# Reworking the head of a two-block kernel: angles, small softmax passes, weight sums and loads

## The chip, the core and the metric

The kernel runs on one core of one Trainium2 chip. The metric is the device time of one execution in microseconds, the median of the runs. Engines are named as in the profile: PE (matmul; PEld is its weight load), DVE (VectorE), ACT (ScalarE), POOL (GpSimd) and SP (SyncE, which issues all DMA). Everything is float32.

## What is computed

Input: 32 sequences of 64 tokens with 512 features, positions, and one condition vector of 512 per sequence. Two blocks follow one another:

```python
# block 0
h = rms_norm(x) * (ln1_w * (1 + cond @ ln1_tw.T))      # per sequence
q, k, v = h @ Wq.T, h @ Wk.T, h @ Wv.T                 # 8 heads of 64, one key/value head
q, k = rope(q, pos), rope(k, pos)                      # angles = pos * 1/10000**(i/32)
x = x + softmax(q k.T / 8) v @ Wo.T
h = rms_norm(x) * (ln2_w * (1 + cond @ ln2_tw.T))
x = x + (silu(h @ Wg.T) * (h @ Wu.T)) @ Wd.T           # 512 -> 2048 -> 512
# block 1
scale, shift = split(cond @ W_ada.T + b_ada)
h = layer_norm(x) * (1 + scale) + shift
q = h @ Wq1.T                                          # 16 heads of 32
c = h @ Wkd.T                                          # latent of 128
k, v = c @ Wku.T, c @ Wvu.T                            # 4 key/value heads
x = x + softmax(rope(q) rope(k).T / sqrt(32)) v @ Wo1.T
```

Attention stays within a sequence of 64 tokens in both blocks. The rope of block 0 takes its positions from the input; that of block 1 uses constant tables.

## The kernel before

Tokens are cut into eight units of 256 (four sequences). A unit lies in SBUF as 128 partitions by 4 feature chunks by 256 tokens. Each unit goes through `attention0` (block 0's attention, and at its end the normed input of the MLP), `mlp`, and `attention1` (block 1).

**MLP.** The three weight matrices (gate, up, down) are cut into eight groups each; every unit goes through these 24 groups in turn. A group is multiplied as a 2 by 2 block product with seven products instead of eight (`SEVEN`). That takes four sums of weight quarters per group. In unit 0, `combine` makes them (lines 211 to 213 on DVE, 214 on POOL; the tile is called `set`, the fourth quarter `a`), and `done_with` stores them (line 219) in a DRAM tile `kept`, called `sums` in the profile. Units 1 to 7 load them from there (line 204). Sets lie in a ring of `MW` = 4 buffers, `a` in a ring of two. `first_products` and `last_products` are gate and up (`gu`, line 723); lines 737, 739, 742 and 749 add the products into `u`, `w` and `c` on DVE, lines 760 to 764 multiply the two, and `down` is line 782.

**Activations.** The seven-product scheme needs sums of the input too: `h` and `hc`, lines 570 to 573, at the end of `attention0`, behind h times the inverse root `r_b` (line 565; 374 is the root on ACT, 375 the reciprocal on DVE).

**Angles.** `angles(u0)` makes sine and cosine of two units' positions, 128 columns at a time: it splits the angle in two parts by the factor 4097, multiplies each by pieces of 1/(2 pi) (line 305), and takes the fraction after each product by adding and subtracting a large constant (`ROUND`, line 300; 301 subtracts, 311 adds up), so that Sin (lines 317, 318) gets a small argument. Line 319 puts the sign on. All but the two Sin runs on DVE. `tables` spreads the result by matmul (`tab`, line 327) and scales it by the inverse root `r_a` to `cs` (lines 333, 334). `angles(0)` runs in the head, `angles(2)` at the end of unit 1's attention0, `angles(4)` and `angles(6)` in the attention0 of units 3 and 5. Note that unit 1's attention0 runs partly in the head too.

**Softmax.** `softmax` works on 128 rows by 8 groups of 64 keys: maximum (line 426), subtract (428), Exp (429), sum (431) and reciprocal (432), then p times sm on POOL (433). `turned` transposes p on PE (`pp`, line 439), ACT copies it (`pT`, 440), `cx` is p times v (549, 692), copied as `cT` (558, 701), and `output` projects it (`po`, line 402 of `project`) and adds x on DVE (452).

**Order.** Jobs are generators that yield planned costs; `Order.run` interleaves them. The head (attention0 of units 0 and 1, with the condition's projections between) and the tail (attention1 of units 6 and 7) are "lean": there one works with more buffers and shares work out, since no MLP runs beside it. In between, `mlp(u)` runs together with attention0 of unit u+1 and with attention1 of earlier units. A scheduler then fixes each engine's instruction order. DMA is all issued by SP in order. The weights of block 1 and x of units 2 to 4 are asked for when the head has been built:

```python
    for w, key in ((wq1, "wq1"), (wkd, "wkd"), (wkv1, "wkv1"), (wo1, "wo1")):
        nc.sync.dma_start(w, a[key])
    for u in range(2, XB):
        load_x(u)
    combine(0)
    combine(1)
```

In `attention1`, line 598 multiplies h by the scale on POOL, 602 multiplies by the inverse root `r_c` on DVE and 603 adds the shift on POOL. The last weight group of the down product and both tail jobs close the kernel; the last `output` stores two halves of unit 7.

Of the kernel before, what the change touches and what calls it, by code (L numbers as in the profile page):

```python
# [17 lines left out]
P = 128  # L18
# [27 lines left out]
ROUND = 12582912.0  # L46
TWO_PI = float(np.nextafter(np.float32(2 * np.pi), np.float32(0)))
# [44 lines left out]
def two_blocks(ctx: ExitStack, tc: tile.TileContext, a: dict, out: bass.AP):  # L92
# [31 lines left out]

    spread = fixed("spread", [P, US, P])
# [11 lines left out]
    nc.gpsimd.memset(eps1, EPS1)  # L137

# [68 lines left out]
    def combine(n):  # L207

        if n < len(sequence) and sequence[n][1] < NP:
            t, a21 = sets[n], odd[n]  # L210
            nc.vector.tensor_tensor(t[:, 0], a21, t[:, 6], ALU.add)
            nc.vector.tensor_tensor(t[:, 1], t[:, 0], t[:, 4], ALU.subtract)  # L212
            nc.vector.tensor_tensor(t[:, 2], t[:, 4], a21, ALU.subtract)
            nc.gpsimd.tensor_tensor(t[:, 3], t[:, 5], t[:, 1], ALU.subtract)

    def done_with(m, q):
        n = place[m, q]
        if q < NP:
            nc.sync.dma_start(kept[3 * (q % NP) + m], sets[n][:, 0:4])
        load_sets(n + 1 + MW)  # L220
# [58 lines left out]
    def angles(u0):  # L279

        cols = slice(u0 * S, (u0 + 2) * S)

        def some(tag, name, cols=512, bufs=2):
            return work(tag, [P, cols], f"{name}_{u0}", bufs)[:, : 2 * S]

        posi = positions.pop()
        posf, sign = some("u", "posf"), some("v", "sign")
        ang, lo, hi, prod = some("p0", "ang"), some("p0", "lo"), some("pT0", "hi", 512, 1), some("r0", "prod", UT, 1)
        acc, rnd = angle[:, 0, cols], angle[:, 1, cols]
        nc.vector.tensor_copy(posf, posi)  # L290
        nc.vector.tensor_scalar(sign, posf, 0.0, None, ALU.is_ge)
        nc.vector.tensor_scalar(sign, sign, 2.0, -1.0, ALU.mult, ALU.add)
        nc.vector.tensor_tensor(posf, posf, sign, ALU.mult)
        nc.vector.tensor_scalar(ang, posf, freq, None, ALU.mult)
# [4 lines left out]
        def fraction(dst, src):  # L299
            nc.vector.tensor_scalar(rnd, src, ROUND, ROUND, ALU.add, ALU.subtract)  # L300
            nc.vector.tensor_tensor(dst, src, rnd, ALU.subtract)

        first = True
        for piece, turn in ((hi, 0), (hi, 1), (lo, 0), (hi, 2), (lo, 1)):
            nc.vector.tensor_scalar(prod, piece, TURN[turn], None, ALU.mult)
            if first:
                fraction(acc, prod)
                first = False
            else:
                fraction(prod, prod)  # L310
                nc.vector.tensor_tensor(acc, acc, prod, ALU.add)
        nc.vector.scalar_tensor_tensor(acc, lo, TURN[2], acc, ALU.mult, ALU.add)
        nc.vector.scalar_tensor_tensor(acc, ang, TURN[3], acc, ALU.mult, ALU.add)
        fraction(prod, acc)
        nc.vector.tensor_scalar(lo, prod, 0.25, None, ALU.add)
        fraction(hi, lo)
        nc.scalar.activation(acc, hi, AF.Sin, scale=TWO_PI)
        nc.scalar.activation(rnd, prod, AF.Sin, scale=TWO_PI)
        nc.vector.tensor_tensor(rnd, rnd, sign, ALU.mult)
# [79 lines left out]

    def project(ps, w, cols, h):  # L400
        for k in range(KC):
            nc.tensor.matmul(ps, w[:, k, cols], h[:, k, :], start=(k == 0), stop=(k == KC - 1))  # L402
# [18 lines left out]
    def softmax(sc, scale, name, p):  # L421
# [6 lines left out]
        nc.vector.tensor_tensor(p3, s3, mx.unsqueeze(2).to_broadcast(heads), ALU.subtract)  # L428
        nc.scalar.activation(p, p, AF.Exp, scale=scale)
        sm = work("sm", [P, 8], f"sm_{name}", 2)  # L430
        nc.vector.tensor_reduce(sm, p3, AX.X, ALU.add)  # L431
# [11 lines left out]
    def output(u, cT, w, name, last=False):  # L443

        x = x_units[u]
        for h in range(2):
            po = abank(f"po_{name}_{h}").rearrange("p (c t) -> p c t", c=2)
            for c in range(2):
                o = 2 * h + c
                project(po[:, c], w, slice(o * P, (o + 1) * P), cT)  # L450
            part = slice(2 * h, 2 * h + 2)
            nc.vector.tensor_tensor(x[:, part], x[:, part], po, ALU.add)  # L452
            yield 3.4, 2.0 * h
# [5 lines left out]
    def attention0(u, room, early=None, late=None):  # L459
# [48 lines left out]
        for i, part in enumerate((a_, b_)):  # L508
            for hh in range(2):
                to = slice((2 * i + hh) * HALF0, (2 * i + hh + 1) * HALF0)  # L510
                ins = [t[part].rearrange("p (b s) -> p b s", s=S) for t in (ku, kw)]
                nc.vector.tensor_tensor(kb[to, :, hh, :], *ins, ALU.add)
# [14 lines left out]
        for t in range(2):  # L527
# [12 lines left out]
            ps.append(softmax(sc, HD0**-0.5, f"0_{u}_{t}", space(room, "p", 512, f"p0_{u}_{t}")))  # L540
# [24 lines left out]
        nc.vector.tensor_tensor(h, h, all_chunks(r), ALU.mult)  # L565
# [14 lines left out]
    def attention1(u, room):  # L580
# [13 lines left out]
        nc.vector.tensor_tensor(h, x, all_chunks(mean), ALU.subtract)  # L594
        sq = tile4(room, "h", f"sq1_{u}") if lean else work("sq", [P, KC, UT], f"sq1_{u}", 1)
        nc.scalar.activation(sq, h, AF.Square)
# [5 lines left out]
        nc.vector.tensor_tensor(h, h, all_chunks(r), ALU.mult)  # L602
        nc.gpsimd.tensor_tensor(by_seq(h), by_seq(h), per_seq(t1, u), ALU.add)
# [62 lines left out]
        def scores(t, h_):  # L666
# [12 lines left out]
            return softmax(sc, HD1**-0.5, name, space(room, "p", 512, f"p{name}"))  # L679
# [128 lines left out]

    def mlp(u):
        for q in range(u * NP, (u + 1) * NP):  # L810
            gate = first_products(0, q)
# [26 lines left out]
    def early():  # L838
        angles(0)
        for z in (kblk0[0], vblk0[0], kblk0[1], vblk0[1], *vblk1):  # L840
            nc.gpsimd.memset(z, 0.0)
# [25 lines left out]
    for w, key in ((wq1, "wq1"), (wkd, "wkd"), (wkv1, "wkv1"), (wo1, "wo1")):  # L867
        nc.sync.dma_start(w, a[key])
    for u in range(2, XB):
        load_x(u)  # L870
# [137 lines left out]
```

## Time and profile before

| what | value |
|---|---|
| median of three runs | 1091.65 us (1091.65 to 1093.0) |
| profiled execution | 1091.63 us, its span 1089.9 us, mean granted PE clock 0.989 |
| busy: PE, PE loads | 1033.7 us (95%), 951.4 us (87%) |
| busy: DVE, POOL, ACT | 586.3 us (54%), 432.5 us (40%), 317.6 us (29%) |
| DMA | 198.45 MB, mean 182 GB/s |
| head, 0 to 78 us | PE busy 60.2 us |
| tail, 1048 to 1090 us | PE busy 34.4 us |

Span is the time between the first and the last instruction of the profiled execution. A line of the timeline gives start, length, engine, source line, operation, out<-in with sizes, and in brackets the idle time before it with the instruction that ended it. "x8" says that eight instructions were drawn together.

### The profile page before, as it was taken

The page shows a single profiled execution, that of the slowest core. Times are in us where ns is not written, and L with a number is a line of the kernel's source. Part 1 is how long each engine was busy: PE and PEld are TensorE (multiplying, and loading weights), DVE is VectorE, ACT ScalarE, POOL GpSimd, SP SyncE. Part 2 cuts the span into 40 slices and gives each one's busy share as a digit, 9 for nine tenths or more (in the row PEclk, how much of TensorE's full clock was granted, in tenths as well). Part 3 has the DMA queues.
Part 4 walks back from the last instruction along what each step waited for, and adds up shares of the span by engine and source line. Part 5 has one row for each costly group of instructions (what it writes and reads, how often), then busy time and mean ns, then how long its engine had stood idle before and what let it go on. Part 6 is the DMA issues. An engine that isn't in the chain of part 4 may idle for free.

```text
span 1089.9 us, 20180 instructions
## 1 busy us (share of the span) xinstructions
PE 1033.7 (95%) x7940; PEld 951.4 (87%) x7940; DVE 586.3 (54%) x1362; ACT 317.6 (29%) x648; POOL 432.5 (40%) x509
## 2 busy tenths in 40 slices
PE   6799899999999999999999998999999999999898
PEld 4679899989999988998988997998999989998776
DVE  5977566554455468333675249443465354235553
ACT  2231022244314234223333222144314242122422
POOL 2334444444245345225434235434335334245531
PEclk9899999999999999999999999999999999999999
DMA  9426786525666264555555374445655266762001
GB/s 332 190 84 205 261 280 221 203 103 204 214 217 218 105 227 180 186 188 203 181 195 186 132 271 162 137 169 203 220 205 204 102 228 217 281 232 79 1 20 39
DMA packets 68109, 198.45 MB, mean 182 GB/s; under 512 B 7216, under 2 KB 15152, under 8 KB 67504
## 3 DMA queue, kind: packets, MB, share of 16 engines
q1 hardware_dynamic: 68016, 197.17, 51.4%
q8 instruction: 63, 1.03, 0.4%
q14 instruction: 30, 0.25, 0.1%
HBM read 180.37 MB, written 16.78 MB: 181 GB/s over the span
## 4 chain that ended last, share of the span: by engine, by line
PE 74%; DVE 9%; DMA 8%; POOL 2%; ACT 2%; issue 2%; SPq 0%; ACTq 0%; DVEq 0%; POOLq 0%
PE gu L723 29%; PE down L782 15%; PE po L402 9%; PE q L402 9%; DMA set<-sums 5%; DMA set<-in_wmlp 3%; PE sc L671 2%; PE pp L439 2%; PE lat L402 1%; PE sc L533 1%; PE cx L549 1%; PE cx L692 1%; PE kv L402 1%; DVE sm L431 1%; PE tab L327 1%
## 5 line engine op out<-in xcount | busy, mean ns | idle before, releaser
L723 PE MATMUL gu<-h,set 128*128 128x128 f32 x2048 | 290.7, 277 | 16.1 <-DVE c L742 6.3
L723 PEld LDWEIGHTS gu<-h,set 128*128 128x128 f32 x2048 | 260.2, 192 | 26.6 <-issue 12.8
L723 PE MATMUL gu<-hc,set 128*128 128x128 f32 x1536 | 215.4, 276 | 2.7 <-DVE set L212 1.9
L723 PEld LDWEIGHTS gu<-hc,set 128*128 128x128 f32 x1536 | 193.2, 193 | 5.2 <-DVE set L212 2.8
L761 POOL TENSOR_TENSOR act<-c,c 128x384 f32<-128x384 f32 x64 | 63.8, 997 | 232.6 <-DVE c L749 152.6
L782 PE MATMUL down<-td,set 128*128 128x128 f32 x1024 | 138.4, 278 | 3.2 <-DMA set<-sums 2.6
L782 PEld LDWEIGHTS down<-td,set 128*128 128x128 f32 x1024 | 126.5, 194 | 5.4 <-issue 3.0
L782 PE MATMUL down<-act,set 128*128 128x128 f32 x768 | 109.8, 278 | 1.8 <-DMA set<-in_wmlp 1.7
L735 ACT COPY e<-gu 128x128 f32<-128x128 f32 x128 | 33.8, 265 | 266.7 <-PE gu L723 266.6
L402 PE MATMUL po<-cT,wo 128*128 128x256 f32 x480 | 109.8, 381 | 1.4 <-ACT cT L558 1.4
L749 DVE TENSOR_TENSOR c<-gu,u 128x256 f32<-128x256 f32 x128 | 53.7, 422 | 104.9 <-PE gu L723 104.0
L782 PEld LDWEIGHTS down<-act,set 128*128 128x128 f32 x768 | 98.2, 192 | 8.2 <-issue 3.5
L737 DVE TENSOR_TENSOR u<-e,gu 128x128 f32<-128x128 f32 x128 | 35.7, 280 | 126.0 <-ACT e L735 125.6
L402 PEld LDWEIGHTS po<-cT,wo 128*128 128x128 f32 x480 | 89.3, 191 | 13.9 <-ACT cT L558 2.1
L419 POOL TENSOR_TENSOR qT<-u_q,v_q 128x512 f32<-128x512 f32 x30 | 38.1, 1269 | 113.1 <-DVE v_q L418 108.3
L433 POOL TENSOR_TENSOR p<-p,sm 128x512 f32<-128x512 f32 x40 | 42.0, 1059 | 98.5 <-DVE sm L432 79.8
L818 ACT ACT_TABLE_LOAD x33 | 42.3, 1283 | 68.4 <-DVE c L749 68.1
L402 PE MATMUL q<-h,wqkv 128*128 128x256 f32 x256 | 60.2, 387 | 0.2 <-ACT r_a L374 0.2
L452 DVE TENSOR_TENSOR x<-x,po 128x512 f32<-128x512 f32 x32 | 22.0, 687 | 71.0 <-PE po L402 71.0
L402 PEld LDWEIGHTS q<-h,wqkv 128*128 128x128 f32 x256 | 48.2, 194 | 7.1 <-issue 0.6
L402 PE MATMUL q<-h,wq 128*128 128x256 f32 x224 | 50.7, 379 | 0.1
L763 POOL TENSOR_TENSOR td<-act 128x256 f32<-128x256 f32 x64 | 47.5, 742 | 4.8
(226 smaller groups left out, 1443.8 us busy)
## 6 DMA issues: line engine op xcount, KB each, us to landing
set<-sums SPq DMA_DIRECT2D x168, 512.0 KB, 5.5
set<-in_wmlp SPq DMA_DIRECT2D x192, 384.0 KB, 4.6
sums<-set SPq DMA_DIRECT2D x24, 512.0 KB, 3.0
mod<-in_mod SPq DMA_DIRECT2D x8, 512.0 KB, 10.0
x<-in_x SPq DMA_DIRECT2D x8, 512.0 KB, 9.2
out_x<-x SPq DMA_DIRECT2D x16, 256.0 KB, 2.0
a<-in_wmlp SPq DMA_DIRECT2D x24, 128.0 KB, 2.5
wo<-in_wo SPq DMA_DIRECT2D x2, 1024.0 KB, 11.0
```

Of the source, the lines that this page charges most:

```text
L402: nc.tensor.matmul(ps, w[:, k, cols], h[:, k, :], start=(k == 0), stop=(k == KC - 1))
L419: nc.gpsimd.tensor_tensor(dst, cut(u, every), cut(v, every), ALU.add)
L433: nc.gpsimd.tensor_tensor(p3, p3, sm.unsqueeze(2).to_broadcast(heads), ALU.mult)
L452: nc.vector.tensor_tensor(x[:, part], x[:, part], po, ALU.add)
L723: nc.tensor.matmul(ps, w[:, slot, k * P : (k + 1) * P], b[of][:, k], start=start and k == 0, stop=k == 1, skip_group_check=True)
L735: nc.scalar.copy(e, ps[:, 0])
L737: nc.vector.tensor_tensor(u2, e, ps[:, 1], ALU.add)
L749: nc.vector.tensor_tensor(c.rearrange("p (a b) t -> p a b t", b=2)[:, :, 1], ps[:, 2:4], u2.unsqueeze(1).to_broadcast([P, 2, HT]), ALU.add,)
L761: nc.gpsimd.tensor_tensor(act[:, 1:4], gate[:, 1:4], c[:, 1:4], ALU.mult)
L763: nc.gpsimd.tensor_tensor(td[:, 0:2], act[:, 1:3], act[:, 0:2], ALU.subtract)
L782: nc.tensor.matmul(sums_of[u][p][:, c], w[:, slot, c * P : (c + 1) * P], b[of], start=q % NP == 0 and i % 2 == 0 and c == 0, stop=q % NP = ...
L818: nc.scalar.activation(gate[2][:, 0], gate[0][:, 0], AF.Silu)
```

## The change

- Eleven matmuls of 128x128 on the constant `ones` stand first on PE (`WARM`).
- `combine` of the first two sets runs on POOL; each `combine` issues the store of its sums itself.
- `angles` has 12 DVE operations and ten on ACT; products, rounding and summation run over five pieces at once; the cosine comes from Sin with a bias of pi/2, the sign from ACT.
- `by_row` shares h times r between DVE and POOL in lean units; the mean's subtraction and the shift of `attention1` are cut in halves there, and half of `kblk` goes to POOL.
- `softmax` of the second tile of lean units: the maximum, times minus the scale, is the bias of eight Exp of 128x64, which also sum up.
- The last output goes in four parts instead of two.
- Weights of block 1 and x of units 3 and 4 are asked for within the list of the MLP's products.

```diff
+WARM = 11
...
+    idle = bank("at", "idle")
+    for _ in range(WARM):
+        nc.tensor.matmul(idle[:, :P], ones, ones, start=True, stop=True)
...
             t, a21 = sets[n], odd[n]
-            nc.vector.tensor_tensor(t[:, 0], a21, t[:, 6], ALU.add)
-            nc.vector.tensor_tensor(t[:, 1], t[:, 0], t[:, 4], ALU.subtract)
-            nc.vector.tensor_tensor(t[:, 2], t[:, 4], a21, ALU.subtract)
+            e = nc.gpsimd if n < 2 else nc.vector
+            e.tensor_tensor(t[:, 0], a21, t[:, 6], ALU.add)
+            e.tensor_tensor(t[:, 1], t[:, 0], t[:, 4], ALU.subtract)
+            e.tensor_tensor(t[:, 2], t[:, 4], a21, ALU.subtract)
             nc.gpsimd.tensor_tensor(t[:, 3], t[:, 5], t[:, 1], ALU.subtract)
+            m, q = sequence[n]
+            nc.sync.dma_start(kept[3 * q + m], t[:, 0:4])
 
     def done_with(m, q):
-        n = place[m, q]
-        if q < NP:
-            nc.sync.dma_start(kept[3 * (q % NP) + m], sets[n][:, 0:4])
-        load_sets(n + 1 + MW)
+        load_sets(place[m, q] + 1 + MW)
...
         nc.vector.tensor_copy(posf, posi)
-        nc.vector.tensor_scalar(sign, posf, 0.0, None, ALU.is_ge)
-        nc.vector.tensor_scalar(sign, sign, 2.0, -1.0, ALU.mult, ALU.add)
-        nc.vector.tensor_tensor(posf, posf, sign, ALU.mult)
-        nc.vector.tensor_scalar(ang, posf, freq, None, ALU.mult)
+        nc.scalar.activation(ang, posf, AF.Abs, scale=freq)
         nc.vector.scalar_tensor_tensor(lo, ang, 4097.0, ang, ALU.mult, ALU.subtract)
         nc.vector.scalar_tensor_tensor(hi, ang, 4097.0, lo, ALU.mult, ALU.subtract)
         nc.vector.tensor_tensor(lo, ang, hi, ALU.subtract)
 
-        def fraction(dst, src):
-            nc.vector.tensor_scalar(rnd, src, ROUND, ROUND, ALU.add, ALU.subtract)
-            nc.vector.tensor_tensor(dst, src, rnd, ALU.subtract)
...
-        for piece, turn in ((hi, 0), (hi, 1), (lo, 0), (hi, 2), (lo, 1)):
-            nc.vector.tensor_scalar(prod, piece, TURN[turn], None, ALU.mult)
...
-                fraction(prod, prod)
-                nc.vector.tensor_tensor(acc, acc, prod, ALU.add)
+        for k, (piece, turn) in enumerate(((hi, 0), (hi, 1), (hi, 2), (lo, 0), (lo, 1))):
+            nc.scalar.mul(prods[:, k], piece, TURN[turn])
+        nc.vector.tensor_scalar(rnds, prods, ROUND, ROUND, ALU.add, ALU.subtract)
+        nc.vector.tensor_tensor(prods, prods, rnds, ALU.subtract)
+        nc.vector.tensor_reduce(acc, prods.rearrange("p k c -> p c k"), AX.X, ALU.add)
         nc.vector.scalar_tensor_tensor(acc, lo, TURN[2], acc, ALU.mult, ALU.add)
         nc.vector.scalar_tensor_tensor(acc, ang, TURN[3], acc, ALU.mult, ALU.add)
-        fraction(prod, acc)
-        nc.vector.tensor_scalar(lo, prod, 0.25, None, ALU.add)
-        fraction(hi, lo)
-        nc.scalar.activation(acc, hi, AF.Sin, scale=TWO_PI)
-        nc.scalar.activation(rnd, prod, AF.Sin, scale=TWO_PI)
-        nc.vector.tensor_tensor(rnd, rnd, sign, ALU.mult)
+        nc.vector.tensor_scalar(rnds[:, 0], acc, ROUND, ROUND, ALU.add, ALU.subtract)
+        nc.vector.tensor_tensor(f, acc, rnds[:, 0], ALU.subtract)
+
+        cos, sin = angle[:, 0, cols], angle[:, 1, cols]
+        nc.scalar.activation(hi, f, AF.Abs)
+        nc.scalar.activation(ang, posf, AF.Sign)
+        nc.scalar.activation(cos, hi, AF.Sin, scale=-TWO_PI, bias=quarter)
+        nc.scalar.activation(lo, f, AF.Sin, scale=TWO_PI)
+        nc.vector.tensor_tensor(sin, lo, ang, ALU.mult)
...
+    def by_row(h, r, lean):
+
+        for e, part in ((nc.vector, slice(0, 2)), (nc.gpsimd, slice(2, 4))) if lean else ((nc.vector, slice(0, 4)),):
+            e.tensor_tensor(h[:, part], h[:, part], r.unsqueeze(1).to_broadcast(list(h[:, part].shape)), ALU.mult)
...
-    def softmax(sc, scale, name, p):
+    def softmax(sc, scale, name, p, lean=False):
...
+        if lean:
+            nc.vector.tensor_scalar(mx, mx, -scale, None, ALU.mult)
+            for h in range(8):
+                nc.scalar.activation(
+                    p3[:, h], s3[:, h], AF.Exp, bias=mx[:, h : h + 1], scale=scale, accum_out=sm[:, h : h + 1]
+                )
+        else:
...
+        n = 1 if last and u == NU - 1 else 2
+        for h in range(KC // n):
...
-            part = slice(2 * h, 2 * h + 2)
-            nc.vector.tensor_tensor(x[:, part], x[:, part], po, ALU.add)
+            part = slice(n * h, n * h + n)
+            nc.vector.tensor_tensor(x[:, part], x[:, part], po[:, :n], ALU.add)
...
-                nc.vector.tensor_tensor(kb[to, :, hh, :], *ins, ALU.add)
+                e = nc.gpsimd if "lean" in room and hh else nc.vector
+                e.tensor_tensor(kb[to, :, hh, :], *ins, ALU.add)
...
+    later = {
+        7: lambda: (nc.sync.dma_start(wkd, a["wkd"]), nc.sync.dma_start(wkv1, a["wkv1"])),
+        8: lambda: nc.sync.dma_start(wq1, a["wq1"]),
+        9: lambda: nc.sync.dma_start(wo1, a["wo1"]),
+        10: lambda: load_x(3),
+        14: lambda: load_x(4),
+    }
...
+            if q in later:
+                later[q]()
...
-        angles(0)
+        angles(0, ("hc", "hc"))
...
-    for w, key in ((wq1, "wq1"), (wkd, "wkd"), (wkv1, "wkv1"), (wo1, "wo1")):
-        nc.sync.dma_start(w, a[key])
-    for u in range(2, XB):
-        load_x(u)
+    load_x(2)
```

Here n counts sets in the order of use, q counts the MLP's groups over all units (eight per unit), and `room` is a job's own buffers.

## The prediction

> **What bounds the kernel now.** I read the page first, then the busy time by stretch, then the timeline of the stretches where PE is not full.
>
> ```profile
> PE 1033.7 (95%) x7940; PEld 951.4 (87%) x7940; DVE 586.3 (54%) x1362; ACT 317.6 (29%) x648; POOL 432.5 (40%) x509
> ```
>
> ```profile
> 0.00:78.00 78.00, 60.24 (x401) 47.59 (x402) 58.43 (x124) 20.88 (x34) 25.72 (x38) 0.91 0.58 212
> 78.00:180.00 102.00, 93.25 (x762) 89.93 (x761) 66.45 (x187) 20.24 (x47) 39.50 (x56) 0.98 0.69 236
> 180.00:650.00 470.00, 462.53 (x3615) 432.56 (x3614) 241.58 (x565) 146.62 (x291) 190.84 (x220) 1.00 0.54 189
> 650.00:670.00 20.00, 14.98 (x116) 13.68 (x116) 17.72 (x44) 7.51 (x14) 12.05 (x15) 1.00 0.63 220
> 670.00:1000.00 330.00, 325.74 (x2575) 306.02 (x2574) 153.26 (x361) 93.65 (x200) 129.72 (x153) 1.00 0.55 191
> 1000.00:1048.00 48.00, 42.50 (x244) 34.95 (x245) 27.01 (x43) 15.50 (x30) 22.59 (x19) 0.96 0.02 6
> 1048.00:1090.00 42.00, 34.42 (x240) 26.65 (x236) 21.86 (x42) 13.15 (x32) 12.10 (x11) 0.99 0.09 32
> ```
>
> Columns: stretch, length, busy us of PE, PE loads, DVE, ACT, POOL, granted clock, DMA share, GB/s. PE's idle time is 17.8 us in the head, 8.8 in the rest of unit 0, 16.7 from 180 to 1000 (5.0 of it in twenty microseconds), and 13.1 in the tail. The change takes no matmul of the MLP away, so only this idle time, and the chains that make it, can move.
>
> The head is a chain of DVE, ACT and POOL:
>
> ```profile
> 23.77 0.29 DVE L319 TENSOR_TENSOR angle<-angle,sign 128x128 f32<-128x128 f32 x1 [0.38 <-ACT angle L318]
> ...
> 25.60 1.75 DVE L375 RECIPROCAL r_a<-r_a 128x256 f32<-128x256 f32 x1 [1.55 <-ACT r_a L374]
> ...
> 27.55 0.41 DVE L333 TENSOR_TENSOR cs<-tab,r_a 128x256 f32<-128x256 f32 x1
> ...
> 62.16 7.17 PE L402 MATMUL po<-cT,wo 128*128 128x256 f32 x32 [0.63 <-ACT cT L558]
> ...
> 64.47 1.27 DVE L211 TENSOR_TENSOR set<-a,set 128x256 f32<-128x256 f32 x1
> ...
> 74.44 1.75 DVE L375 RECIPROCAL r_b<-r_b 128x256 f32<-128x256 f32 x1 [3.93 <-ACT r_b L374]
> 76.29 1.23 DVE L565 TENSOR_TENSOR h<-h,r_b 128x1024 f32<-128x1024 f32 x1
> ...
> 79.26 0.94 PE L723 MATMUL gu<-hc,set 128*128 128x128 f32 x7
> ```
>
> The angles end at 24.06, and only then do the root's table load (1.28) and r_a run, so cs waits until 27.55. At the other end the MLP waits for hc, which waits for r_b.
>
> The 5 us around 660 us are angles(6) itself, which holds DVE while the MLP wants u, w and c:
>
> ```profile
> 657.14 1.90 POOL L598 TENSOR_TENSOR h<-h,s 128x1024 f32<-128x1024 f32 x1
> 657.29 1.82 DVE L300 TENSOR_SCALAR angle<-prod 128x128 f32<-128x128 f32 x1
> ...
> 660.94 1.13 PE L723 MATMUL gu<-h,set 128*128 128x128 f32 x8 [1.64 <-DVE angle L300]
> ...
> 664.55 1.13 PE L723 MATMUL gu<-h,set 128*128 128x128 f32 x8 [2.04 <-DVE c L742]
> ...
> 667.06 1.16 PE L327 MATMUL tab<-angle,spread 128*128 128x128 f32 x8 [0.49 <-DVE angle L319]
> ```
>
> **What the skill says.** The Trainium skill, "SBUF — State Buffer", section "Who interferes with whom": a VectorE instruction with two SBUF inputs, or a tensor_scalar in its two-port mode, and a GpSimd instruction reading SBUF exclude each other; the later waits the earlier out. The rows agree: L300 takes 1.82 us under POOL's 1.90 against 0.22 alone; L211 1.27 under p times sm against 0.36. I go by the rows: POOL work added beside DVE is not free, it alternates. For the eight Exp of 128x64 there is no row. "ScalarE: Activation LUTs", section "What ACT_TABLE_LOAD costs", gives about 280 ns plus 0.83 per column, some 93 ns overlapped back to back: by estimate 0.24 each, without its accumulator. From the trace: a 64x64 copy takes 0.21, and a bias pointer adds 0.10 (root 0.47 against copy 0.37). I take 0.30; bounds 0.24 and 0.50.
>
> **The change part by part.**
>
> *Idle matmuls.* Eleven on PE before its first work. PE's early work waits for loads, and the first ms_a matmuls run at half rate (3.78 us for eight; 1.89 later) under the cover of the angles. Zero; with the angles gone as cover, up to −1.
>
> *Loads and stores.* Wkd, wkv, wq and wo of block 1 and x(3), x(4) are asked for in products 7 to 14 of the MLP's list, but in the built order SP still issues them ahead of set_4, since nothing holds them there. On SP the second a21 load waits for POOL's first combine, and set_3, x(2) and these loads queue behind it; they land by about 60 us, before the MLP's start at 78. A store goes out right behind its own sum's POOL instruction instead of after the last product; the reload still waits for PE to free the buffer. Unit 0 costs a set load of 5.3 us plus sums against about 4 us of PE per set, and that stays: zero, ±1.
>
> *Angles(0).* 35 DVE operations of 0.23 to 0.29 (9.6 us) and two Sin become 12 on DVE and ten on ACT. Five 128x128 products go to ACT (0.3 each); round, subtract and reduce come as one each of 640 columns (0.5, 0.85, 0.8 by the rows 0.42 at 256, 0.69 at 512, 1.22 at 1024). A Sin table load sits between Abs and Sin on the path (1.28). Together tab comes near 23.1 against 24.1, −1. The larger step: the reciprocal r_a now stands among the angles on DVE, so cs starts at about 24.2, not 27.55.
>
> *Head, onward.* Half of each h times r goes to POOL, and so does half of kblk. The two first combines put six more instructions of 0.73 on POOL, which now idles 14.9 us before its first qT rotation (30.4); the two sets are asked for at 10.6 and 11.5 us and land by about 21 at the 8 to 10 us of the loads around them, so the six end near 25, ahead of the rotation; up to +1 if they alternate with DVE's angle operations. u_q of the second pair moves from 47.4 to about 43.5 (−3.9). The last normalised p of unit 0 moves only by 1, because sets 2 and 3 combine on DVE and lock with POOL there. From its transposes' end (55.6 − 1 = 54.6): copy 0.60, cx 1.13 and 0.33, eight Exp 2.4 between the two cT copies, copy 0.35; po starts at 59.4 against 62.16, −2.75.
>
> *po to the MLP.* Po to r_b is 12.3 us as before, plus 0.5 (angles(2)'s Abs ahead on ACT). From r_b's reciprocal to hc before: 3.1 us. After: the halves on DVE and POOL 1.05 with the lock, and the 640-column round, subtract and reduce of angles(2) (0.5 + 0.85 + 0.8) stand between the hc products in the built order, where before two of 0.22 did: +2.1. PE had 0.43 of other work. Sum −2.75 + 0.5 + 2.1 − 0.43 ≈ −0.6; bounds −3.5 (PE's other work fills) and +1.5.
>
> *Rest of unit 0.* Angles(2) cost PE 0.70 at 93.0 and 0.71 at 100.5: −1.4 returned; two table loads instead of one in its first product, of which some +0.5 reaches PE. ≈ −0.9; −3 to +1.
>
> *Angles(4) and (6).* PE's waits for them sum to 0.9 and 4.2 us. DVE's batch shrinks from 9.6 to 4.5 us, and three instructions can be held by POOL where L300, L301 and L311 were held one by one. But it stands in one piece that waits on ACT in the middle, and an MLP c stands behind it, with PE's last products and ACT's Silu behind that. I take six tenths of 5.0: −3; −5 to +1.
>
> *Tail.* By the built order po of unit 6 now stands behind the transposes of unit 7's first scores on PE, and 16 small Exp on ACT ahead of its pT copies:
>
> ```profile
> 1018.73 2.81 POOL L603 TENSOR_TENSOR h<-h,t 128x1024 f32<-128x1024 f32 x1 [4.37 <-DVE h L602]
> ...
> 1066.30 7.17 PE L402 MATMUL po<-cT,wo 128*128 128x256 f32 x32
> ...
> 1078.86 7.17 PE L402 MATMUL po<-own_mw,wo 128*128 128x256 f32 x32 [0.75 <-ACT own_mw L701]
> ...
> 1086.07 0.69 DVE L452 TENSOR_TENSOR x<-x,po 128x512 f32<-128x512 f32 x1 [2.77 <-PE po L402]
> ```
>
> The halves at 1018 change nothing by alternation (−2 if DVE is first throughout). First po +2.1, of which 0.8 returns behind it because subtract and sum (0.69 each) have left DVE: second po +1.3 to +2.1. The last add is 128x256 (0.42 for 0.69), −0.3, with a smaller store behind. Net +0.8; −2 to +3.
>
> Sum: −0.6 − 0.9 − 3 + 0.8 = −3.7 against the profiled 1091.63 (span 1089.9 and 1.7 around it), which equals the median: 1087.9, a span of 1086.2.
>
> **The rivals.**
>
> *Slower, 1095.* Small Exp as the new bound: at 0.5 each instead of 0.3 po starts 1.6 later in the head (MLP +1.0, with the POOL lock +1.5), the 16 in the tail put the last po at +3, and if ACT's small products also hold angles(6), its idle stays. +1.5 − 0.9 + 3 + 0 ≈ +3.6. It decides from about 0.42 each on. For it: ACT has 34 instructions in 78 us and becomes a link in a chain; against: copy rows of 0.21.
>
> *Much faster, 1082.5.* PE's other work fills the gaps between the hc products, so the head keeps its −3.5, unit 0 gives −1.4, both angle waits go (−5.0), tail +0.8: −9.1. Against: the sums' lock, and a batch in one piece.
>
> *It does not do what it says, 1091.6.* Loads are not later, stores free nothing; head and angles give 2 to 4 that the set loads of unit 0 (5.3 against 4 us) and the tail take back.
>
> **Chances.** A measurement here tells about 0.2%, 2.2 us, from no change: faster is below 1089.5, slower above 1093.8. Forecast 0.55 (own range 1084 to 1091.5; 0.45 faster, 0.10 same), slower rival 0.25 (0.20 slower, 0.05 same), much faster 0.10, no effect 0.10 (0.02, 0.05, 0.03). Faster 0.57, same 0.20, slower 0.23. The range 1081 to 1096 takes in the rivals' values; some 0.07 lies below and 0.1 above.
>
> **What would show it.** Right: cs near 24, po of unit 0 near 59.5, first gu<-hc near 78.7, no PE wait over 1 us near 660, po of unit 7 near 1076. Wrong: Exp of 128x64 above 0.4, L305 at 640 columns or the halves on POOL far over these durations, the extra table load in front of a c, or set loads as PE's releaser in unit 0.

## The result and the profile after

The changed kernel takes 1098.75 us (median of 20 runs, 1091.39 to 1106.08) against 1091.65 us of the kernel before (20 runs). The ratio is 1.0066, with a 95% interval of 1.0049 to 1.0083: 7.1 us slower, where 3.7 us faster was forecast. The profiled execution shown here ran 1101.72 us, 3.0 above the median, its span 1099.9 us, so its differences add up to 10.0 instead of 7.1.

The row of engines, and the busy time by stretch at the same limits as before (stretch, length, busy us of PE, PE loads, DVE, ACT, POOL, then granted clock, DMA share, GB/s):

```profile
PE 1044.4 (95%) x7962; PEld 961.4 (87%) x7962; DVE 562.1 (51%) x1260; ACT 339.4 (31%) x774; POOL 445.0 (40%) x524
```

```profile
0.00:78.00 78.00, 63.28 (x419) 50.77 (x420) 46.35 (x84) 29.15 (x79) 33.49 (x50) 0.91 0.61 212
...
650.00:670.00 20.00, 15.94 (x132) 15.22 (x131) 10.79 (x26) 6.36 (x11) 8.77 (x10) 0.99 0.71 249
...
1048.00:1090.00 42.00, 35.91 (x237) 27.32 (x236) 18.17 (x38) 20.41 (x92) 12.81 (x12) 0.92 0.07 26
```

DVE lost 24 us of work and 102 instructions, as the change says; ACT and POOL took up 22 and 13 us. PE itself is busy 10.7 us longer with 22 instructions more: the eleven idle matmuls, two records each, take 5.1 us of it. No other matmul was added; more than half of the rest lies in the tail, where PE is busy 51.8 us from unit 7's lat to the end, before 48.8. The clock column of the last row shows the reason: 0.92 in the tail, before 0.99.

The span splits into four pieces by marks in the timeline (`lat` is the latent product of `attention1`):

| piece | before | after | difference |
|---|---|---|---|
| start to the first ms_a on PE | 10.1 | 11.4 | +1.3 |
| first ms_a to the first gu<-hc (head) | 69.2 | 70.8 | +1.6 |
| first gu<-hc to unit 7's lat | 954.3 | 956.5 | +2.1 |
| unit 7's lat to the end (tail) | 56.3 | 61.2 | +4.9 |

The first row is when the first loads land. Over all profiles of this study it lies between 10.0 and 11.8 us with no relation to the kernel, so it explains nothing, and times in the head are best counted from ms_a. The third row lies between 947 and 957 us over these profiles, so its 2.1 us say little. The tail stands out: it takes 56.2 to 56.3 us in every profile with the old softmax and two last outputs, except one (57.4).

The head in the timeline of the changed kernel (start, length, engine, line, operation, and the idle time before it with its releaser):

```profile
17.07 1.75 DVE L374 RECIPROCAL r_a<-r_a 128x256 f32<-128x256 f32 x1 [2.05 <-ACT r_a L373]
...
21.80 0.83 POOL L219 TENSOR_TENSOR set<-a,set 128x256 f32<-128x256 f32 x1 [5.31 <-DMA a<-in_wmlp]
...
22.07 0.64 DVE L310 TENSOR_SCALAR turns<-few 128x128 f32<-128x128 f32 x1
...
26.51 1.13 PE L326 MATMUL tab<-angle,spread 128*128 128x128 f32 x8 [1.88 <-DVE angle L318]
...
27.67 0.42 DVE L332 TENSOR_TENSOR cs<-tab,r_a 128x256 f32<-128x256 f32 x1 [1.31 <-PE tab L326]
28.02 3.46 PE L406 MATMUL kv<-h,wqkv 128*128 128x256 f32 x8
...
63.17 7.17 PE L406 MATMUL po<-cT,wo 128*128 128x256 f32 x32 [3.00 <-ACT cT L571]
...
75.50 1.75 DVE L374 RECIPROCAL r_b<-r_b 128x256 f32<-128x256 f32 x1 [0.84 <-ACT r_b L373]
...
77.52 1.75 DVE L402 TENSOR_TENSOR h<-h,r_b 128x512 f32<-128x512 f32 x1
...
82.23 1.16 PE L740 MATMUL gu<-hc,set 128*128 128x128 f32 x8 [0.44 <-DVE hc L585]
```

The reciprocal is out of the way between angles and cs, as forecast: cs follows tab by 1.2 us. But it now stands among the angles and DVE waits 2.05 us for it; then POOL's sums of the first two weight sets start at 21.8 and hold the last short angle operations (L310: 0.64 us for 0.23). PE, idle in front of tab, runs kv at half speed (3.46 us against 1.89 with the new angles alone). And po has waited 3.00 us for an ACT copy, which stands behind eight Exp.

The tail, from the middle of unit 7's attention:

```profile
1056.67 3.62 PE L406 MATMUL q<-own_mw,wq 128*128 128x256 f32 x16
...
1061.13 0.31 ACT L436 ACTIVATE own_h<-sc,mx 128x64 f32<-128x64 f32 x1 [0.35 <-POOL own_h L444]
1061.34 0.19 ACT L436 ACTIVATION_READ_ACCUMULATOR own_h<-sc,mx 128x1 f32 x1
1061.43 0.30 ACT L436 ACTIVATE own_h<-sc,mx 128x64 f32<-128x64 f32 x1
...
1063.17 0.34 ACT L436 ACTIVATE own_h<-sc,mx 128x64 f32<-128x64 f32 x1
...
1064.00 0.66 PE L450 MATMUL pp<-ident,own_h 128*128 128x128 f32 x4 [2.19 <-POOL own_h L444]
1064.08 0.59 ACT L451 COPY pT<-pp 128x512 f32<-128x512 f32 x1
...
1064.72 0.66 PE L709 MATMUL cx<-pT,vblk 128*64 128x128 f32 x8
...
1077.21 7.07 PE L406 MATMUL po<-cT,wo 128*128 128x256 f32 x32
...
1089.40 7.17 PE L406 MATMUL po<-own_mw,wo 128*128 128x256 f32 x32 [0.75 <-ACT own_mw L718]
```

Each Exp with its accumulator read comes 0.29 us after the one before. The transposes that the first pT copy takes were done at 1060.7; it runs at 1064.08, because the eight Exp stand ahead of it. PE has a second wait at the same place: its transposes at 1064.00 wait for POOL's p times sm, which in the new order stands behind a POOL multiplication of 1.90 us (from 1061.05). With the old softmax that multiplication comes after it. Both waits come with the new softmax and end together; no run separates them. Unit 6's po comes 38.5 us after unit 7's lat, before 32.7. The clock in this stretch, in the same columns as above:

```profile
1055.00:1060.00 5.00, 5.00 (x30) 4.10 (x27) 4.75 (x13) 3.66 (x21) 1.68 (x2) 1.00 0.00 0
1060.00:1065.00 5.00, 2.31 (x20) 1.52 (x19) 2.74 (x6) 4.22 (x23) 5.00 (x5) 1.00 0.00 0
1065.00:1070.00 5.00, 4.15 (x29) 2.93 (x27) 0.00 (x0) 1.29 (x4) 1.17 (x2) 0.54 0.00 0
1070.00:1075.00 5.00, 4.88 (x42) 3.53 (x39) 3.16 (x6) 2.57 (x11) 0.00 (x0) 0.77 0.01 2
```

PE is busy for only 2.31 of five microseconds, and in the next ten it is granted 0.54 and 0.77 of its clock: a score matmul of unit 7 takes 0.63 us at 1068.67 and 0.38 at 1072.36.

### The profile page after: what moved, and what is told of

Read it like the earlier page. It is cut to its first block, busy times and chain, and to the rows that moved or that the text cites. A ratio compares the mean times of both kernels' runs of the same rounds, so it can differ in the third digit from the quotient of the medians.

```text
span 1099.9 us, 20279 instructions
## 1 busy us (share of the span) xinstructions
PE 1044.4 (95%) x7962; PEld 961.4 (87%) x7962; DVE 562.1 (51%) x1260; ACT 339.4 (31%) x774; POOL 445.0 (40%) x524
## 4 chain that ended last, share of the span: by engine, by line
PE 74%; DMA 9%; DVE 8%; POOL 3%; ACT 2%; issue 2%; SPq 1%; ACTq 0%; DVEq 0%; POOLq 0%
PE gu L740 29%; PE down L799 15%; PE po L406 9%; PE q L406 8%; DMA set<-sums 5%; DMA set<-in_wmlp 3%; PE sc L688 2%; PE pp L450 2%; PE cx L709 1%; PE lat L406 1%; PE sc L546 1%; PE cx L562 1%; PE kv L406 1%; DMA a<-in_wmlp 1%; DMA x<-in_x 1%
## 5 line engine op out<-in xcount | busy, mean ns | idle before, releaser
L846 ACT ACT_TABLE_LOAD x33 | 42.3, 1283 | 64.2 <-DVE c L766 63.9
L464 DVE TENSOR_TENSOR x<-x,po 128x512 f32<-128x512 f32 (+1 forms) x34 | 22.3, 656 | 74.4 <-PE po L406 74.4
L846 ACT ACTIVATE c<-gu 128x128 f32<-128x128 f32 x64 | 17.8, 277 | 108.4 <-DVE c L766 105.9
```

What stands on the lines that cost most here:

```text
L464: nc.vector.tensor_tensor(x[:, part], x[:, part], po[:, :n], ALU.add)
L846: nc.scalar.activation(gate[2][:, 0], gate[0][:, 0], AF.Silu)
```

## The experiments

All ratios are to the kernel before, in runs on the same chip, with the 95% interval. Five chips (A to E) were used, and ratios from one chip compare best. "After" in the table means the changed kernel, whose own 1.0066 comes from a chip that is not on record; the nearest to it on chip A is the one with nothing shared (1.0064). The new angles alone were run on B and E, not on C and D.

| chip | kernel | median us | ratio | interval |
|---|---|---|---|---|
| A | after, old softmax in the tail | 1090.75 | 1.0001 | 0.9980 to 1.0023 |
| A | after, old softmax everywhere | 1092.09 | 1.0008 | 0.9994 to 1.0023 |
| A | after, idle matmuls in the tail | 1092.73 | 1.0027 | 1.0009 to 1.0044 |
| A | after, nothing shared | 1098.38 | 1.0064 | 1.0043 to 1.0085 |
| B | before, new softmax | 1092.95 | 1.0027 | 1.0013 to 1.0042 |
| B | before, new angles | 1085.37 | 0.9954 | 0.9934 to 0.9973 |
| B | before, idle matmuls in the head | 1091.29 | 1.0011 | 0.9991 to 1.0031 |
| B | before, idle matmuls in the head, tail sharing, four outputs | 1088.33 | 0.9986 | 0.9972 to 0.9999 |
| C | angles, sums and stores and loads moved | 1091.35 | 1.0003 | 0.9988 to 1.0018 |
| C | angles, sharing | 1089.33 | 0.9983 | 0.9967 to 1.0000 |
| C | angles, first idle matmuls | 1086.18 | 0.9961 | 0.9938 to 0.9983 |
| C | angles, tail sharing, four outputs | 1085.09 | 0.9948 | 0.9928 to 0.9968 |
| D | angles, sums on POOL | 1090.09 | 0.9992 | 0.9972 to 1.0013 |
| D | angles, stores and loads moved | 1088.83 | 0.9987 | 0.9973 to 1.0002 |
| D | angles, new softmax in the head | 1088.87 | 0.9989 | 0.9974 to 1.0004 |
| D | angles, tail sharing, four outputs, idle matmuls in the head | 1088.47 | 0.9984 | 0.9968 to 1.0000 |
| E | before, new angles (again) | 1087.35 | 0.9973 | 0.9959 to 0.9988 |
| E | angles, stores and loads moved (again) | 1090.50 | 1.0000 | 0.9979 to 1.0021 |

"Angles" means the kernel before with the new `angles` alone.

### The small Exp and the clock in the tail

The theory formed from the trace: each small Exp costs what was forecast, but where they stand PE runs out of work, and its clock falls.

```diff
-            return softmax(sc, HD1**-0.5, name, space(room, "p", 512, f"p{name}"), lean and h_ == 1)
+            return softmax(sc, HD1**-0.5, name, space(room, "p", 512, f"p{name}"))
```

> The changed kernel with the old softmax in the tail only (block 1, units 6 and 7); the head keeps the eight Exp. Theory A (the small Exp stand ahead of the pT copies on ACT, PE idles, and its granted clock falls): po of unit 6 starts some 33 us after the lat of unit 7 instead of 38.5, the clock of the tail stays at 1.0, and the median falls by 4 to 5, from 1098.75 to about 1094. Theory B (the work shared out between DVE and POOL is what costs): within 1 of 1098.75. Theory C (the angles batch costs): the same, within 1.

This edit alone takes the ratio from 1.0066 to 1.0001, some 7 us. In its timeline unit 7's lat stands at 1037.85 and unit 6's po 32.7 us later, as in the kernel before:

```profile
1070.54 4.80 PE L406 MATMUL po<-cT,wo 128*128 128x256 f32 x21
```

The tail takes 55.7 us, against 56.3 before and 61.2 after: 5.5 us by the trace, the rest within the interval. The same edit in both places:

> The changed kernel with the old softmax everywhere. Theory A: as with the old softmax in the tail, and po of unit 0 in the head starts about 1.7 us earlier besides (2.4 of Exp between its two cT copies against 0.6), so a median of 1092 to 1093. Theory B and C: 1098 or so.

It gives 1.0008, no better than the tail alone; in the head it gained no more than the intervals hide.

The next run leaves the Exp in place and gives PE something to do in the wait they make:

```diff
         query(1)
+        if u == NU - 1:
+            fill = bank("gu", "fill")
+            for _ in range(14):
+                nc.tensor.matmul(fill[:, :P], ones, h[:, 0, :P], start=True, stop=True)
         yield 3.4, 4.5
```

> The changed kernel with 14 further matmuls of 128x128 on PE behind unit 7's last query product (their result is read by nobody). Theory A: they lie in PE's wait for the small Exp (2.2 and 0.9 us idle), take 3.1 us there, and the granted clock at the scores of unit 7 stays at 1.0 instead of 0.54 to 0.77; po of unit 6 comes about 3 us earlier, the median falls to about 1095.5 to 1096.5. If the low clock is not due to PE's own idle time, the time stays or rises by up to 3.

It adds work and is faster: 1.0027. The stretch that holds its fill and the three behind it:

```profile
1055.00:1060.00 5.00, 5.00 (x36) 4.71 (x35) 4.53 (x11) 4.59 (x28) 4.03 (x4) 1.00 0.00 0
1060.00:1065.00 5.00, 4.29 (x43) 3.34 (x43) 0.20 (x1) 2.67 (x11) 3.44 (x4) 1.00 0.01 3
1065.00:1070.00 5.00, 4.59 (x46) 2.91 (x42) 3.94 (x8) 3.92 (x19) 0.24 (x1) 1.00 0.00 2
1070.00:1075.00 5.00, 4.15 (x21) 3.73 (x22) 2.14 (x7) 4.62 (x24) 2.89 (x3) 1.00 0.00 0
```

The clock stays at 1.00 and the tail takes 58.1 us: by these two profiles 3.1 of the 4.9 us were the clock. The other 1.8 are the delay that the new softmax makes itself, less the 0.6 that the four outputs give. The clocks of all runs agree: the mean granted clock is 0.984 over the 20 runs of the changed kernel, 0.988 over those with the fill and over those with the old softmax in the tail, and 0.990 over those of the kernel before on chip A. The Trainium skill states the rule ("TensorE: Matmul & The Clock Gate", Part 1): the clock is halved after a window of about 3.4 us without PE work and comes back after as long a busy one; its Part 4 says that transposes do not count like other matmuls. The trace fits both: behind unit 7's last query product no product but transposes runs for 4.4 us in the changed kernel and 1.9 before; with the fill, 1.3 us lie between it and the next. Counted with the transposes, PE's longest pause there is 2.19 us. How long a wait has to be does not come out of these traces: in the kernel before, a wait of 2.30 us (at 509.6) is followed by four microseconds at a clock of 0.61, so less than 3.4 us can do, and below, one of 3.15 us leaves the clock at 1.00.

The new softmax on the kernel before, without the rest:

```diff
+        if lean:
+            nc.vector.tensor_scalar(mx, mx, -scale, None, ALU.mult)
+            for h in range(8):
+                nc.scalar.activation(p3[:, h], s3[:, h], AF.Exp, bias=mx[:, h : h + 1], scale=scale, accum_out=sm[:, h : h + 1])
```

> The kernel before with nothing but the new softmax (head and tail). Theory A (small Exp ahead of the pT copies, then the low clock): the tail from unit 7's lat to the end grows from 56.3 to 61 us with the granted clock near 0.65 for some ten microseconds, po of unit 0 in the head starts 1 to 2 us later: +5.5 to +7 in all, so 0.5 to 0.65% over the kernel before. Rival (the Exp hurt only in the tail as it is reordered by the shared h times r and shift): +2 or less.

1.0027, half of what was expected, and not clear of the 2 us of the rival (that the Exp hurt only where the sharing has reordered the tail). Another run settles that: with nothing shared, the changed kernel's tail still takes 61.3 us. The tail here takes 59.3 us (+3.0), and the clock falls for a shorter time:

```profile
1055.00:1060.00 5.00, 2.77 (x15) 2.04 (x16) 0.95 (x3) 3.33 (x16) 4.34 (x4) 0.71 0.00 0
1060.00:1065.00 5.00, 5.00 (x53) 3.63 (x53) 2.32 (x5) 2.54 (x9) 0.00 (x0) 0.95 0.00 0
```

The gap is much the same (4.8 us), and yet the clock stays low for some 3.3 us where it did for 6.9. So the loss from one gap differs with when the clock falls and returns; one profile for each kernel does not say how often each case comes. The runs of the changed kernel spread over 14.7 us, those of the kernel before over 7.5, and the changed kernel's fastest run had the highest mean clock (1091.39 us, 0.990), its slowest the lowest (1106.08 us, 0.975). That fits, but was not tested further.

### What the angles give, and where

> The kernel before with nothing but the new angles. The prediction's own terms (waits of PE in units 3 and 5 shrink by 3, unit 0 by 1): 3 to 4 below the kernel before. What the trace of the changed kernel suggests (fewer but longer instructions, which alternate with POOL and stand in front of a c or of the hc products; PE's waits 6.4 us there against 6.6): within 1.5 of the kernel before, either way.

0.9954, and 0.9973 on a second chip (below): 2.9 to 5.0 us. The size is near the forecast's (3.9 for the angles outside the head), the place is not, so it is luck that the sizes agree. In its timeline:

```profile
16.11 1.75 DVE L370 RECIPROCAL r_a<-r_a 128x256 f32<-128x256 f32 x1 [1.44 <-ACT r_a L369]
...
24.16 1.13 PE L322 MATMUL tab<-angle,spread 128*128 128x128 f32 x8 [0.90 <-DVE angle L314]
...
25.33 0.42 DVE L328 TENSOR_TENSOR cs<-tab,r_a 128x256 f32<-128x256 f32 x1 [1.31 <-PE tab L322]
```

The tables are hardly earlier (24.16, before 24.11; counted from ms_a 13.7 against 14.0), but cs is, by 2.2 us, or 2.6 counted from ms_a, because the reciprocal is already done. Head: 66.4 us against 69.2 (67.1 in the second profile). From the first gu<-hc to unit 0's lat: 127.8 against 131.3 (129.2 in the second profile). The 131.3 is high: three other profiles with the old angles have 129.4 to 130.3, and in this one PE waits 2.63 us for a set load at 123.7. So some 2 us of this are the angles. The units behind it gain nothing: from unit 0's lat to unit 3's 470.8 against 471.2, and from there to unit 7's 351.2 against 351.9. The waits there look like this:

```profile
381.74 1.22 PE L718 MATMUL gu<-h,set 128*128 128x128 f32 x4 [3.32 <-ACT c L813]
...
384.46 1.91 PE L718 MATMUL gu<-h,set 128*128 128x128 f32 x8
...
659.15 1.13 PE L718 MATMUL gu<-h,set 128*128 128x128 f32 x8 [3.15 <-DVE c L737]
```

Angles(4) now makes one wait of 3.32 us where there were 1.55, 0.45 and 0.42, and 660 has one of 3.15 where there were 1.64, 2.04 and 0.49. Behind the first PE runs at half speed (eight matmuls in 1.91 us, 1.06 otherwise), behind the second it does not. In the changed kernel's profile both of its waits there (3.32 and 3.08 us) are followed by four microseconds at a clock of 0.64 and 0.57, where before it stays at 1.00. A batch in one piece trades several short waits for one long one.

### What takes it back

```diff
+            e = nc.gpsimd if n < 2 else nc.vector
+            e.tensor_tensor(t[:, 0], a21, t[:, 6], ALU.add)
...
+            nc.sync.dma_start(kept[3 * q + m], t[:, 0:4])
...
+            if q in later:
+                later[q]()
```

> The kernel before with the new angles and, besides, the first two sums on POOL, the stores issued by combine and the later loads. Theory D (these six POOL instructions alternate with the end of the angles on DVE, 0.64, 0.71 and 0.84 us for 0.23 to 0.29 in the changed kernel, and PE, kept waiting, runs at a lower clock): tab comes 1 to 2 later after ms_a than with the angles alone (13.7), and the kernel loses 2 to 4 of the 4.9 us that these gain: ratio about 0.998. Rival (the sums are hidden): ratio 0.995 as with the angles alone.

1.0003: the whole gain is gone. Its head takes 70.6 us instead of 66.4. The end of its angles:

```profile
21.29 0.72 POOL L215 TENSOR_TENSOR set<-a,set 128x256 f32<-128x256 f32 x1 [4.37 <-DMA a<-in_wmlp]
21.36 0.80 DVE L305 SCALAR_TENSOR_TENSOR few<-few 128x128 f32<-128x128 f32 x1
...
22.19 0.63 DVE L306 TENSOR_SCALAR turns<-few 128x128 f32<-128x128 f32 x1
...
22.85 0.71 DVE L307 TENSOR_TENSOR turns<-few,turns 128x128 f32<-128x128 f32 x1
...
26.06 2.05 PE L322 MATMUL tab<-angle,spread 128*128 128x128 f32 x8 [4.48 <-DVE angle L314]
```

Three DVE operations take 2.14 us where they took 0.81 with the angles alone, each ending some 0.1 us behind a POOL instruction, which is the exclusion that the Trainium skill's "SBUF — State Buffer", section "Who interferes with whom", describes. PE then waits 4.48 us and does tab in 2.05 us, against 1.13. The three edits apart:

> The kernel before with the new angles and only the first two sums on POOL (stores and loads as before). Theory D (POOL's six instructions alternate with the last angle operations on DVE): the whole loss of the three moves together, ratio 0.999 to 1.001, tab 15 us after ms_a. Rival (the order of stores and loads costs): ratio 0.995 to 0.996.

> The kernel before with the new angles, the stores issued by combine and the later loads, all sums of DVE's kind where they were. Theory D: the same as the angles alone, ratio 0.995 to 0.996, tab 13.7 us after ms_a. Rival: 0.999 or more.

0.9992 and 0.9987. POOL's sums show the same delay (tab 15.0 us after ms_a, 13.7 without them; head 68.7). It is not there every time: in the two profiles of the changed kernel with the fill and with nothing shared, the sets land when the short angle operations are over, and tab comes 13.0 and 13.2 us after ms_a. The stores and loads were expected to be free, and their tab is not late (13.6), but they are not free either; since they ran on another chip than the angles alone, both ran once more side by side:

> The new angles alone once more, beside the stores and loads on one chip: if the gain of 0.46% holds from chip to chip, a ratio of 0.994 to 0.997; if the last four ratios near 0.9987 were the chip's, 0.998 or more.

> The new angles with stores issued by combine and later loads, on the same chip as the angles alone. Theory D (only POOL's sums cost): within 0.1% of these. If the moved stores and loads cost: 0.2 to 0.35% above them.

0.9973 and 1.0000: 0.27% again, though the intervals touch. In the two pairs of profiles the head of the moved stores and loads is 1.2 and 1.1 us longer (67.7 and 68.1 against 66.4 and 67.1). Theory D, that only POOL's sums cost, is not borne out; by what path the moved stores and loads cost stays open.

Sharing between DVE and POOL was tried from both sides:

```diff
-        nc.vector.tensor_tensor(h, h, all_chunks(r), ALU.mult)
+        by_row(h, r, "lean" in room)
```

> The changed kernel with h times r, the kblk additions, the mean's subtraction and the shift back in whole instructions on the engine they had before. Theory B: the alternation of DVE and POOL goes, median 1094 or less. Theory A: it returns about 0.7 at the first h times r, 1.0 at the c that waited 2.3 us near 166 us, and costs up to 0.5 at the start of lat in the tail: 1097 to 1098.

> The kernel before with the new angles and the work shared between DVE and POOL (h times r, kblk, mean, shift). Theory E: sharing lengthens the hc products in the head and the c of unit 0 (by about 1 us each) and gains 0.6 in the tail, net +1 to +2: ratio 0.996 to 0.9975. If it is what takes the gain of the angles back: ratio 0.999 or more.

Taken out of the changed kernel it gives 1.0064, no difference; in that profile unit 0 reaches its lat in 129.9 us instead of 131.6, but po of the head runs at half rate at first (8.86 us for 7.17), which hides what sharing costs or gives. Added to the angles it gives 0.9983, above the 0.9948 to 0.9961 of its neighbours on chip C. Its trace has the c that waits at 160.7 us for 2.19 (1.25 with the angles alone), and unit 0 takes 130.8 us to its lat, against 127.8. It is a small loss beside the MLP, below what a whole-kernel comparison settles.

> The kernel before with the new angles and the eleven idle matmuls. Theory: they end at 6.2 us, and whether the clock is still high when ms_a starts depends on when the first condition weights land, so ms_a takes 3.78 or 1.99 us; nothing waits for it longer than the table load, so the same as with the angles alone, ratio 0.994 to 0.997. If PE's early clock counted: 0.993 or less.

0.9961: the idle matmuls at the start do nothing that can be measured.

The small Exp in the head alone:

> The kernel before with the new angles and the eight small Exp in the head only. The eight stand between the two cT copies in the head, 2.3 us for one Exp of 0.63, so po of unit 0 and the MLP start 1 to 2 later: ratio 0.9965 to 0.9975. If the subtraction and sum saved on DVE outweigh it (the prediction's sign for the head): 0.9955 or less.

0.9989, above the 0.9965 to 0.9975 expected, though on a chip without the angles alone. The copy that feeds po, with the angles alone and with the Exp:

```profile
57.94 0.36 ACT L553 COPY cT<-cx 128x256 f32<-128x256 f32 x1
58.36 7.17 PE L397 MATMUL po<-cT,wo 128*128 128x256 f32 x32 [1.14 <-ACT cT L553]
```

```profile
58.99 0.69 ACT L560 COPY cT<-cx 128x256 f32<-128x256 f32 x2
59.73 8.76 PE L397 MATMUL po<-cT,wo 128*128 128x256 f32 x32 [2.72 <-ACT cT L560]
```

cx was done near 57.0 in both; the Exp hold the copy, and po starts 1.4 us later, 1.8 counted from ms_a. And po itself takes 1.6 us longer: PE has waited 2.72 us, and its clock is 0.5 for the first three. So in this profile the small Exp do in the head what they do in the tail, and the MLP starts 3.4 us later (head 69.8 us against 66.4). The profile of the changed kernel with the fill has the same at po (8.57 us for 7.17), the changed kernel's own has not (7.17), so this is a loss that comes in some executions only.

### A version that beats both

> The kernel before with the new angles, the shared h times r, mean and shift in the tail alone, and the last output in four parts. By the traces 0.6 and 0.65 less than the angles alone: about 1084, ratio 0.994, and below both kernels. If the tail's reordering costs: 0.996.

The new angles, the sharing in the tail only and the four outputs: 1085.09 us, ratio 0.9948 (0.9928 to 0.9968). It is faster than the kernel before and the changed one. Its tail takes 55.6 us, 0.7 less than before, and that is the four outputs: with the sharing and two outputs it takes 56.3. What the sharing gives lies ahead of it (between the lats of units 5 and 6: 42.3 to 42.6 us instead of 42.9 to 43.2); against the angles alone (0.9954, another chip) the difference is below what can be told.

Idle matmuls in the head, where the kernel before has a clock of 0.56 between 50 and 60 us, were tried on three bases:

```diff
+        if i == 3:
+            for _ in range(16):
+                nc.tensor.matmul(ps[:, 256 : 256 + P], ones, ones, start=True, stop=True)
         rows = work("latT1"
```

> The kernel before with 16 matmuls of 128x128 on PE, read by nobody, behind the last condition product of the head, where PE idles 5.2 us. If PE's idle time sets its clock, the granted clock from 50 to 60 us rises from 0.56 to near 1.0, the transposes, scores and cx behind it take about half (2 to 2.5 us of the chain), and the kernel gains 1 to 2. If the clock there comes from something else, 0 to +1.

> The kernel before with these 16 matmuls, the shared h times r, mean subtraction and shift in the tail only, and the last output in four parts. By the traces 0.6 in the tail for the sharing, 0.6 for the output, 1 to 2 for the head: 2 to 3 below the kernel before. If the gains are hidden: the same as it.

> The best version so far (new angles, sharing in the tail, last output in four parts) with 16 idle matmuls in the head's PE gap. If the low clock at 45 to 55 us is worth what the spans of the earlier trial suggest (1.2): 1084, ratio 0.9938. If the chain there does not hang on PE: the same, 0.9948.

On the kernel before the clock rose to 1.00 from 50 to 60 us, and the time did not change (1.0011). With the tail's edits it is 0.9986, and on the best version 0.9984, not better than the 0.9948 without. Only the first was run on one chip with its base, so the last two say little. The profile of the last shows one reason: the clock is 1.00 from 50 to 60 us, but PE then waits 2.5 us, and po takes 8.83 us instead of 7.17:

```profile
60.56 8.83 PE L405 MATMUL po<-cT,wo 128*128 128x256 f32 x32 [2.50 <-ACT cT L562]
```

There the low clock was moved, not removed. In the other two profiles po takes 7.17 and the head is 1.2 and 1.7 us shorter than the 69.2 of the kernel before, which the intervals neither show nor exclude. So whether filling pays in the head stays open.

## Why the prediction was wrong

- **Tail, forecast +0.8 (−2 to +3), measured +4.9.** The price of one Exp was right: 0.29 us with its accumulator read, 0.30 taken. The place was right too: they stand ahead of the pT copies. The term missing from the sum was PE's clock, 3.1 us. I had the half rate at the first ms_a in front of me and treated it as a matter of the start. Missing as well is POOL's multiplication, which now stands ahead of p times sm; its share is not separated. The slower rival named the right part, the small Exp, but not the clock: it has them decide by their length, from 0.42 us each on, and they decided at 0.29.
- **Head, cs at 24.2; measured 27.67.** Of these 3.5 us, 1.3 are the later first load, which is scatter. I moved cs forward by the reciprocal's stay and tab by another 1.0, though the same reciprocal now stood within the angles and waited for ACT: with the angles alone tab gained 0.3 and cs 2.6 from ms_a on, not 1.0 and 3.3. Another 1.4 before tab are POOL's first sums, which I had priced at up to +1 and then left out of the sum; they ran from 21.8 us on, right beside the last angle operations on DVE.
- **Head, the Exp between the cT copies.** I let 2.4 us of them stand in the chain and still came to −2.75 for po, from the early cs and the early p. From ms_a on, po gained 0.3 in the changed kernel. The runs show +1.8 for the Exp alone. The gain they were set against was there with the angles alone (po 4.2 earlier from ms_a on), and with the Exp added to these, po was 2.4 earlier, near the forecast; in the changed kernel most of this was lost, 1.4 of it by POOL's sums. What the sum lacked here as well is the clock: where it falls at po, po takes 1.4 to 1.7 us longer.
- **po to the MLP, forecast +2.1 between r_b and the first hc products; measured +1.9** (6.8 us from the end of r_b's root to gu<-hc, before 4.9). This step held.
- **Angles(4) and (6), −3; measured none.** From unit 0's lat to unit 3's, four profiles with the old angles take 470.1 to 471.8 us, and the new angles 468.3 to 473.5. I had named the batch in one piece with a c behind it, and then counted DVE time, not the longest wait. PE's two waits became 3.3 and 3.1 us.
- **Rest of unit 0, −0.9; measured −2.1 to −3.5 with the angles alone,** some 2 against the other profiles with the old angles, and nothing of it in the changed kernel (131.6 us for 131.3). With nothing shared it has 129.9, so sharing takes part of it; the rest is open.
- **Stores and loads, zero ±1; measured about +0.3%** (3 us) in two comparisons, one of them across chips; cause open.
- **The first idle matmuls, zero: held.** The last output, forecast −0.3, gave 0.6 to 0.7 by the trace, and the shared tail, forecast at nothing, some 0.6.

In sum the angles gain 3 to 5 us, and the softmax, the sums with their stores and loads, and probably the sharing take back more. The forecast had the durations of these nearly right; it put PE's clock at nothing, and what POOL's sums do to the DVE operations beside them. These two were the steps that failed, the clock in the tail first of all.

## What to carry over

Work moved to an idle engine is not off the path: ask what stands behind it in that engine's order, and which instructions of another engine it holds while it runs. Before a chain on other engines grows, look how long PE already waits in it; in this kernel a gap of 4.4 us without products other than transposes cost 3.1 us more than itself, and 14 idle matmuls took that back. And test a change of many parts one part at a time: here one part was worth more than the rest, with the rest taken off.

## What was unexpected

- An Exp of 128x64 with an accumulator shows as two records, 0.31 and 0.19 to 0.25 us, and a new one starts every 0.29 us, so eight take 2.3 us against 0.63 for one Exp of 128x512.
- A sum over five strided pieces of 128 columns took 1.25 us, a 128x512 sum over contiguous keys 0.69.
- Five operations merged into one are held as one: the subtraction of 640 columns took 0.81 us in the head, and 2.40 beside a POOL instruction of 2.15 in unit 3.
- The same wait can be followed by a low clock in one execution and not in another: behind 3.00 us without work, po in the head took 7.17 us in the changed kernel and 8.57 in the one with the tail's fill. Of the twenty profiles, four have such a slow po (8.57 to 8.86).
